# Projecting q one step earlier, spacing a feed-forward, and issuing the second attention's stores from one queue, in a two-layer transformer kernel

## The chip, the cores and the metric

The kernel runs on one core of a Trainium2 chip. The metric is device time in microseconds, from launch to end, median of several runs. The engines are TensorE (PE, with its weight loads shown as PEld), VectorE (DVE), ScalarE (ACT), GpSimd (POOL) and SyncE (SP), which only issues DMAs.

## The reference

The input x has two batches of 1024 rows of 256 features. Two layers follow each other, and each has an attention and a feed-forward; each of the four parts adds the layernorm of its result to x.

```
x = x + LN(L0_attn(LN(x)))   # 16 heads of 128, 1024 keys, weights are codes times block scales
x = x + LN(L0_ffn(LN(x)))    # silu(x Wg * gs) * (x Wu * us) @ Wd * ds, 704 hidden
x = x + LN(L1_attn(LN(x)))   # 16 heads of 16, causal
x = x + LN(L1_ffn(LN(x)))    # 16 experts of 128, top 8 of them weighted, and a shared one of 256
```

## The kernel before, in words

**Precision.** Most operands of a matmul are split into a high and a low 16-bit part: ACT writes the high part, and POOL or DVE subtracts it from the float32 value to give the low part.

**The first attention** sets the pace. `l0_attn` (L704 onward) lists heads of a batch in halves of 512 query rows; a half has four steps, one for each 128 query rows. There are 256 steps in all, 128 for each batch. In step s, `l0_soft` (L627) multiplies q by k into a score tile `pss` of 128x1024, of which there are two; DVE takes the maximum (L631), ACT the exponential `e` (L633). One step later `l0_split` casts it to `hl` (ACT L641, POOL L642) and SP transposes it by DMA into `PT` (L654). Six steps after the scores, `l0_av` (L669) multiplies by v; the result OT goes through `l0_out` (L687).

Each head's projections are put into steps by the function `on`, relative to the first step s of the half that they serve: k (first half only) in steps s-4 and s-3, q in step s-2, v in s+2 and s+3. `l0_qk` is four matmuls (L540) into a tile of `psp` and then the split into two halves: for q, ACT casts (L569 and L572) and POOL subtracts (L573), or ACT and DVE (L545 to L547). q and k have two buffers each. For some heads k and v are stored to DRAM and loaded later for the second half.

**The rest is laid beside it.** `at(step, functions, rate)` puts a list of functions into steps, one each `rate` steps. The feed-forward of the first layer (`ffn`) is such a list for each 512 rows: six times `gu` (gate and up, L873), an empty place, `down` (L889) for the first 256 rows, and the same with two empty places for the others. `down` needs the six hidden tiles `ff_h`, whose low part POOL writes (L881). Three lists are placed at steps 120, 146 (first batch) and 246 (second) at rates of 0.55 and 0.65; the last list runs after the first attention.

The second attention's projections (`l1_qkv`: qk at L981, v at L1019) of the first batch are placed at steps 136 and 160. A qk result is split into a high and low part `l_sq` (`l_sqs` in the second batch), stored to DRAM three times (k as high, high, low; q as high, low, high), and loaded back into `l_k` or `l_q` (L998), stacked so that one matmul does all products of high and low parts. The two copies of the high part are issued by ACT right after its cast (L989); the low part is issued by SP (L992) some ticks later (`QK_LAG`), and the loads a few ticks after that. The work of the second attention itself (`l1_plan`: peaks L1048, scores L1100, `av` L1128) is one list that `between` feeds into the steps at about 1.5 places each from `L1_AT` on. A half begins only when the one before it is through.

**The tail.** After step 256 a planner with made-up time units (`t`) mixes the last feed-forward, the second batch's second attention and the experts (`moe`, L1313 and L1344). `C_FFN` holds the unit at which the last feed-forward begins and its spacing.

**Who orders what.** PE's order is the program's own. On the other engines and in SP's queue a scheduler orders instructions from their place in the program and priorities, so that moving one instruction can reorder others. Every engine works through its instructions in order. SP's queue holds the transposes, loads and stores of everything else too.

Of the kernel before, what the change touches and what calls it, by code (L numbers as in the profile page):

```python
# [22 lines left out]
H0, HD0 = 16, 128  # L23
# [37 lines left out]
L1_W = (100, 104)  # L61
FFN_AT = ((120, 146), 0.55)
FFN1_AT = (246, 0.65)
QKV_AT = ((136, 160), 2.2)
L1_AT = (149, 173)
L1_RATE = (1.6, 1.5)
LAST = 6
EW_AT = (262, 253, 251, 256, 262, 259, 311, 295)
# [5 lines left out]
MOE_LAG = 6  # L74
MUL_DVE = 0.5
C_L1 = 3.2
C_FFN = (20.0, 2.02)
C_QKV = (6.0, 16.0, 3.4)
C_ST = (18.0, 26.0)
C_X3 = 13.09  # L80
# [7 lines left out]
class Net:  # L88
# [615 lines left out]
    def l0_attn(self, filler, between):  # L704


        heads, n, g0 = [], 256, H0 - LAST
        for b in range(B):
            for p, half, hs in ((2 * b, 0, range(g0)), (2 * b, 0, range(g0, H0)), (2 * b, 1, range(H0 - 2, H0)),
                                (2 * b + 1, 1, range(g0, H0 - 2))):  # L710
                for h in hs:
                    heads.append(dict(p=p, b=b, h=h, half=half, PT=[], end=False, keep=g0 <= h < H0 - 2,
                                      w=lambda p=p, h=h: self.wq[p, h // 2]))
                    if h < g0:
                        heads.append(dict(heads[-1], half=1, PT=[]))
                heads[-1]["end"] = p % 2 == 1 or (half == 0 and h == H0 - 1)
        jobs = {}

        def on(s, f):
            jobs.setdefault(s, []).append(f)  # L720

        def tiles(st, *names):
            for x in names:
                if x == "q":
                    st["q"] = self.work.tile([P, 2, 512], F16, name="q", bufs=2)
                else:
                    self.set_kv(st, x, self.new_kv(x))

        deq = {}

        def weights(pair):
            with self.gate():
                deq[pair] = self.l0_weights(pair)

        def reload(ps, pair):
            with self.gate():
                self.l0_reload(ps, pair)

        def reload_o(ps, pair):
            with self.gate():  # L740
                self.l0_reload_o(ps, pair)

        for j, st in enumerate(heads):
            p, h, half, s = st["p"], st["h"], st["half"], 4 * j
            if p % 2 == 1:
                on(s - (5 if h == H0 - 3 else 2), lambda st=st: (tiles(st, "q"), self.l0_qk(st, 0, 1)))
                on(s - 4, lambda st=st: self.kv_load(st, "k"))
                on(s + 2, lambda st=st: self.kv_load(st, "v"))
            elif half == 0:
                on(s - 4, lambda st=st: (tiles(st, "k"), self.l0_qk(st, 1, 0)))  # L750
                on(s - 3, lambda st=st: self.l0_qk(st, 1, 1))
                on(s - 2, lambda st=st: (tiles(st, "q"), self.l0_qk(st, 0, 0)))
                on(s + 2, lambda st=st: (tiles(st, "v"), self.l0_v(st, 0)))
                on(s + 3, lambda st=st: self.l0_v(st, 1))
            else:
                first = heads[j - (1 if h < g0 else 2)]
                on(s - 2, lambda st=st, h0=first: (tiles(st, "q"), self.set_kv(st, "k", h0["k_t"]), self.l0_qk(st, 0, 1)))
                on(s + 3, lambda st=st, h0=first: self.set_kv(st, "v", h0["v_t"]))
            if h % 2 == 0 and (p % 2 or half == 0):
                g = h // 2  # L760
                if p == 0:
                    if g:
                        on(s - 8, lambda g=g: weights(g))
                    for k, dt in enumerate((-6, -5, -2, -1, 2)):
                        if g or k >= 3:
                            on(s + dt, lambda g=g, k=k: deq[g][k]())
                else:
                    on(s - 8, lambda p=p, g=g: reload(p, g))
                    on(s + 1, lambda p=p, g=g: reload_o(p, g))
        on(4 * next(j for j, st in enumerate(heads) if st["h"] == H0 - 2) + 4, self.l0_bias)  # L770
        ready = self.ln_start(self.x0)
        with self.tc.issue_after(ready.ins):
            deq[0] = self.l0_weights(0)
            for f in deq[0][:3]:
                f()
        ps = self.psp.tile([P, 512], F32, name="psp")
        for _ in range(WARM):
            self.nc.tensor.matmul(ps[:, :256], self.zero[:, :P], self.zero[:, :256], start=True, stop=True)
        out_todo = []
        for s in range(-4, n + 3 + L0_LAG + 4):  # L780
            if 0 <= s < n:
                st, qt = heads[s // 4], s % 4
                if qt == 0:
                    st["sum"] = self.small.tile([P, 4], F32, name="sum")
                self.l0_soft(st, qt)
            if 1 <= s <= n:
                self.l0_split(heads[(s - 1) // 4], (s - 1) % 4, s - 1)
            a = s - 3 - L0_LAG
            av = [lambda i=i: self.l0_av(heads[a // 4], a % 4, i) for i in range(2)] if 0 <= a < n else []
            todo = jobs.pop(s, [])  # L790
            if out_todo:
                todo += [f for f in (out_todo.pop(0),) if f]
            if s >= 0:
                todo += filler(s)

            if a % 4 == 0 and av:
                todo = todo[: (len(todo) + 1) // 2] + av[:1] + [lambda: between(s, 0)] + todo[(len(todo) + 1) // 2 :] + av[1:]
            else:
                k = len(todo)
                todo = (todo[: -(-k // 3)] + av[:1] + [lambda: between(s, 0)] + todo[-(-k // 3) : -(-2 * k // 3)]  # L800
                        + av[1:] + todo[-(-2 * k // 3) :])
            for f in todo + [lambda: between(s, 1)]:
                f()
            if av and a % 4 == 3:
                out_todo = [None] * OUT_LAG + [lambda t2=t2, st=heads[a // 4]: self.l0_out(st, t2) for t2 in range(2)]
        assert not jobs, jobs
# [46 lines left out]
    def ffn(self, b, half):  # L853

        nc, w = self.nc, self.work
        st = {}
# [26 lines left out]
        def down(c):  # L883
            ps = self.new_ps()
            for t in range(2):
                for i in range(NI):
                    rows = P if i < 5 else 64
                    for j in range(2):
                        nc.tensor.matmul(ps[:, 256 * t : 256 * t + 256],  # L889
                                         st["h", c, i][:rows, j, t * P : (t + 1) * P], self.fd[:rows, i, :],  # L890
                                         start=(i == 0 and j == 0), stop=(i == NI - 1 and j == 1))
            pv = ps.rearrange("p (t f) -> p t f", t=2)
            y = self.new_y()
            nc.vector.tensor_mul(y, pv, self.ds_bc.unsqueeze(1).to_broadcast([P, 2, D]))
            self.ln_add(1, b, 4 * half + 2 * c, y)

        todo = [lambda i=i: gu(0, i) for i in range(NI)]
        todo += [lambda: None, lambda: down(0)]
        todo += [lambda i=i: gu(1, i) for i in range(NI)]
        return todo + [lambda: None, lambda: None, lambda: down(1)]  # L900


    def l1_weights(self):
# [51 lines left out]
    def l1_qkv(self, b, m):  # L955

        nc, p = self.nc, self.work
        st = {}

        def qk(which, c):  # L960
            n = "qk"[which]
            if b:
                if which == 1:
                    st["sq", c] = p.tile([P, 2, 2, 512], F16, name="l1_sqs", tag="e", bufs=3)
                sq = st["sq", c][:, which, :, :]
            else:
                self.n_sq += 1
                tag, bufs = (("hl_w", 1), ("st", 2), ("st", 2))[self.n_sq % 3]
                sq = p.tile([P, 2, 512], F16, name="l1_sq", tag=tag, bufs=bufs)
            st[n, c] = p.tile([P, 4, 512], F16, name="l1_" + n, bufs=(L1Q_BUFS, 4)[which])  # L970
            if which == 1:
                d = self.k_d1[self.n_kd % 4]
                self.n_kd += 1
            else:
                d = self.dram.tile([2, 50, 4, 512], F16, name="l1_qd", bufs=4)
            ps = self.new_ps()
            col = which * D + m * P
            k = 0
# [5 lines left out]
            bias = self.bqk[:, 2 * which + m : 2 * which + m + 1]  # L984
            self.scaled(sq[:, 0, :], sq[:, 1, :], ps, SC1 / WS1, bias)

            parts = [d[:, 16 * i : 16 * i + 16, :, :].rearrange("g r j t -> g (r j) t") for i in range(3)]
            for i in (0, 2 - which):
                nc.scalar.dma_start(parts[i], sq[:, 0, :])  # L989

            def store():
                self.qk_mark = nc.sync.dma_start(parts[1 + which], sq[:, 1, :])  # L992

            def load():
                rows = 48 + 2 * which
# [4 lines left out]
            todo = [store, load]  # L1000
# [26 lines left out]
        todo = []  # L1027
# [358 lines left out]
    def run(self):  # L1386
        nc, tc = self.nc, self.tc
        with ExitStack() as ctx:
# [62 lines left out]
            for g in range(2):  # L1451
                at(FFN_AT[0][g], self.ffn(0, g), FFN_AT[1])
                at(QKV_AT[0][g], qkv[0, 0][3 * g : 3 * g + 3] + qkv[0, 1][3 * g : 3 * g + 3], QKV_AT[1])
            at(FFN1_AT[0], self.ffn(1, 0), FFN1_AT[1])
# [13 lines left out]
            def between(s, end):  # L1468


                if not end:
                    g = (done[0] >= n_h[0]) + (done[0] >= n_b0)
                    go = g < 2 and s >= L1_AT[g]
                    acc[0] = min(acc[0] + L1_RATE[g], 3.0) if go else 0.0
# [163 lines left out]
```

## Time and profile before

| What | Value |
|---|---|
| Median of three runs | 1785.34 us (1783.87 to 1785.71) |
| The profiled execution's own time | 1787.07 us |
| Its span, first to last instruction | 1785.3 us |
| Mean granted TensorE clock | 0.977 |
| DVE, ACT, POOL busy | 71%, 62%, 50% of the span |
| First attention's scores (L627), first to last | 27.3 to 1247 us |
| Stores of l_sq and l_sqs by ACT / by SP | 32 / 16 |

A profile is one execution. "Busy" counts an engine's own instructions, not its waits or its issuing of DMAs. A wait reads as: engine, tile and line that waited <- engine, tile and line that ended the wait: us in total, times, longest us. PEclk is the share of the full TensorE clock that was granted in a stretch of time.

### The profile page before, as it was taken

Reading aid. Unit: us, or ns where it says so; the run is one execution under the profiler, and the core shown is the slowest. Engines: PE = TensorE matmul, PEld = TensorE weight load, DVE = VectorE, ACT = ScalarE, POOL = GpSimd, SP = SyncE. Lnnn points to the kernel's source line nnn. Section 1 sums busy time; section 2 is a strip of 40 time slices with the busy share of each in tenths; the row PEclk is TensorE's granted clock in tenths of the full one; section 3 lists DMA queues with packets and bytes.
Section 4 is the critical chain, followed back from the end, with each engine's and each line's share of the span. In section 5 each row is a group of like instructions: output and inputs, shape, how many; then the busy total and the mean of one; then the engine's idle time right before and its main releaser. Section 6 shows DMA issues by size and latency. Waiting matters only on the chain.

```text
span 1785.3 us, 35902 instructions
## 1 busy us (share of the span) xinstructions
PE 1608.3 (90%) x13903; PEld 1075.3 (60%) x13903; DVE 1262.1 (71%) x2535; ACT 1109.0 (62%) x1856; POOL 897.0 (50%) x701
## 2 busy tenths in 40 slices
PE   5999999999889888999988889889868898999998
PEld 2566666666556565665555555545656576776877
DVE  5766767676978669565876667886758478775666
ACT  4787787777666655677576777667433444555432
POOL 3666667656666645445445434465343233333444
PEclk9999999999999999999999999999989999999999
DMA  5886988998976975695667766776784322111120
GB/s 125 193 195 156 193 189 184 240 215 179 238 170 164 144 136 117 111 158 128 141 152 179 194 182 152 184 190 162 245 122 105 111 64 67 49 43 45 59 72 13
DMA packets 635316, 257.24 MB, mean 144 GB/s; under 512 B 574916, under 2 KB 615656, under 8 KB 634888
## 3 DMA queue, kind: packets, MB, share of 16 engines
q1 hardware_dynamic: 630984, 250.74, 61.9%
q10 hardware_dynamic: 4160, 4.19, 0.7%
q8 instruction: 109, 1.79, 0.4%
q14 instruction: 63, 0.52, 0.1%
HBM read 76.66 MB, written 35.33 MB: 63 GB/s over the span
## 4 chain that ended last, share of the span: by engine, by line
PE 46%; DVE 24%; ACT 10%; DMA 8%; issue 7%; POOL 2%; SPq 1%; ACTq 0%; DVEq 0%; POOLq 0%
PE pss L627 10%; PE psa L669 9%; PE psp L1313 6%; DVE l_nm L1059 4%; DVE nm L631 4%; PE psp L540 4%; ACT e L633 3%; PE psa L1344 3%; PE psy L1128 2%; ACT hl L641 2%; PE psp L687 2%; DMA pre_ew<-hl_w 2%; PE pss L1100 1%; DVE ln_st L140 1%; PE psp L584 1%
## 5 line engine op out<-in xcount | busy, mean ns | idle before, releaser
L642 POOL TENSOR_TENSOR hl<-e,hl 128x1024 f16<-128x1024 f32 x231 | 492.6, 2133 | 419.9 <-ACT hl L641 315.3
L669 PE MATMUL psa<-PT,v 128*128 128x256 f16 x3072 | 410.9, 275 | 12.4 <-ACT qk L567 11.2
L631 DVE TENSOR_REDUCE nm<-pss 128x1 f32<-128x1024 f32 x256 | 312.0, 1219 | 142.8 <-PE pss L627 142.1
L627 PE MATMUL pss<-k,q 128*128 128x512 f16 x1536 | 379.5, 382 | 35.8 <-ACT e L1112 8.6
L633 ACT ACTIVATE e<-pss,nm 128x1024 f32<-128x1024 f32 x256 | 285.8, 1117 | 128.5 <-DVE nm L631 100.4
L669 PEld LDWEIGHTS <-v 128*128 128x128 f16 x3072 | 296.9, 99 | 105.0 <-issue 28.8
L641 ACT CAST hl<-e 128x1024 f16<-128x1024 f32 x256 | 268.6, 1049 | 13.1 <-DMA PT<-hl 9.7
L627 PEld LDWEIGHTS <-q 128*128 128x128 f16 x1536 | 145.3, 98 | 183.9 <-issue 37.2
L1059 DVE TENSOR_REDUCE l_nm<-pss 128x2 f32<-128x1024 f32 (+3 forms) x152 | 175.8, 1159 | 29.5 <-PE pss L1053 24.9
L1313 PEld LDWEIGHTS <-ew 128*128 128x128 f16 x1728 | 166.1, 99 | 49.6 <-issue 26.3
L1330 POOL TENSOR_TENSOR m_h<-m_t,m_h 128x256 f16<-128x256 f32 x144 | 97.4, 678 | 175.2 <-ACT m_h L1329 173.1
L540 PE MATMUL psp<-xa,wr 128*128 128x512 f16 x488 | 127.9, 386 | 12.6 <-DVE k L552 4.0
L1313 PE MATMUL psp<-xa,ew 128*128 128x256 f16 x1032 | 129.9, 277 | 8.5 <-ACT l_yT L1160 5.1
L1329 ACT CAST m_h<-m_t 128x256 f16<-128x256 f32 x144 | 58.1, 404 | 106.1 <-POOL m_t L1328 40.4
L1320 DVE SCALAR_TENSOR_TENSOR m_t<-m_t,psp 128x256 f32<-128x256 f32 x121 | 50.3, 416 | 95.6 <-ACT m_t L1319 95.1
L573 POOL TENSOR_TENSOR OT<-qk,OT 128x512 f16<-128x512 f32 x64 | 81.3, 1271 | 58.1 <-issue 29.6
L696 DVE SCALAR_TENSOR_TENSOR acc<-psp,r,acc 128x256 f32<-128x256 f32 x224 | 97.1, 474 | 18.9 <-PE psp L687 18.4
L1344 PE MATMUL psa<-ed,m_h 128*128 128x256 f16 x756 | 105.1, 276 | 0.0
L1319 ACT ACTIVATE m_t<-psp 128x256 f32<-128x256 f32 x121 | 46.4, 383 | 89.4 <-PE psp L1313 81.1
L1344 PEld LDWEIGHTS <-m_h 128*128 128x128 f16 x864 | 85.5, 99 | 10.7
L540 PEld LDWEIGHTS <-wr 128*128 128x128 bf16 x512 | 49.4, 99 | 70.1 <-issue 19.0
L1112 ACT ACTIVATE e1x<-pss 128x1024 f32<-128x1024 f32 (+1 forms) x80 | 75.1, 941 | 22.8 <-PE pss L1107 11.8
(221 smaller groups left out, 2637.4 us busy)
## 6 DMA issues: line engine op xcount, KB each, us to landing
cb<-cT_d SPq DMA_DIRECT2D x32, 512.0 KB
w_c<-in_w_codes SPq DMA_DIRECT2D x8, 1024.0 KB
x_d<-y SPq DMA_DIRECT2D x24, 256.0 KB
xr<-x_d SPq DMA_DIRECT2D x24, 256.0 KB
pre_ew<-hl_w SPq DMA_DIRECT2D x18, 256.0 KB
PT<-hl SPq DMA_TRANSPOSE x256
k_d<-k SPq DMA_DIRECT2D x8, 512.0 KB
v_d<-v SPq DMA_DIRECT2D x8, 512.0 KB
```

The lines of the kernel that those rows point to most:

```text
L540: nc.tensor.matmul(ps, w()[:, 1 - which, kt, hs], self.xT[0, st["b"], c][:, :, 2 * j + kt, :], start=(kt == 0 and j == 0), stop=(kt == 1 a ...
L627: nc.tensor.matmul(ps[:, sl], q[:, a, qs], k[:, bb, sl], start=(a == 0 and bb == 0), stop=(a == 1), skip_group_check=True)
L631: self.nm_mark = nc.vector.reduce_max(nm, ps, axis=AX.X, negate=True)
L633: nc.scalar.activation(e, ps, AF.Exp, bias=nm, accum_out=st["sum"][:, qt : qt + 1])
L641: nc.scalar.copy(hl[:, 0, :], e)
L642: (nc.vector if lo_dve else nc.gpsimd).tensor_sub(hl[:, 1, :], e, hl[:, 0, :])
L669: nc.tensor.matmul(ps, v[:, x, kt, :], PT[:, 8 * y + kt, :], start=(kt == 0 and n == 0), stop=(kt == 7 and n == 2))
L696: nc.vector.scalar_tensor_tensor(ys, pv, r, ys, op0=ALU.mult, op1=ALU.add)
L1059: nc.vector.reduce_max(nms[t][:, i % 2, :, j0 : j0 + nj, c], pv, axis=AX.X)
L1313: nc.tensor.matmul(ps[:, 256 * o : 256 * o + 256], self.ew[e][:, o, a, kt, :], xT[:, sl, 2 * x + kt, :], start=(n == 0), stop=(n == 5))
L1330: nc.gpsimd.tensor_sub(h[:, 1, :], th, h[:, 0, :])
L1344: nc.tensor.matmul(py[:, 256 * t : 256 * t + 256], h[:, a, t * P : (t + 1) * P], self.ed[e][:, w, :], start=False, stop=(e == NE - 1 and t ...
```

## The change

Three things. (1) q of a head is projected three steps before its scores instead of two; k one step earlier as well (s-5 and s-4), except for the very first head. (2) Each feed-forward but the last has two more empty places before each `down`; the constants that place the second attention's projections and its start are moved by some steps (`QKV_AT`, `L1_AT`), and the last feed-forward starts 3 planner units later. (3) ACT issues no store of l_sq or l_sqs any more; all three are issued by SP where it issued the low part. Nothing is added to or removed from the arithmetic.

```
-QKV_AT = ((136, 160), 2.2)
-L1_AT = (149, 173)
+QKV_AT = ((138, 166), 2.2)
+L1_AT = (150, 179)
...
-C_FFN = (20.0, 2.02)
+C_FFN = (23.0, 2.02)
...
             if p % 2 == 1:
-                on(s - (5 if h == H0 - 3 else 2), lambda st=st: (tiles(st, "q"), self.l0_qk(st, 0, 1)))
+                on(s - (5 if h == H0 - 3 else 3), lambda st=st: (tiles(st, "q"), self.l0_qk(st, 0, 1)))
...
             elif half == 0:
-                on(s - 4, lambda st=st: (tiles(st, "k"), self.l0_qk(st, 1, 0)))
-                on(s - 3, lambda st=st: self.l0_qk(st, 1, 1))
-                on(s - 2, lambda st=st: (tiles(st, "q"), self.l0_qk(st, 0, 0)))
+                on(max(s - 5, -4), lambda st=st: (tiles(st, "k"), self.l0_qk(st, 1, 0)))
+                on(max(s - 4, -3), lambda st=st: self.l0_qk(st, 1, 1))
+                on(max(s - 3, -2), lambda st=st: (tiles(st, "q"), self.l0_qk(st, 0, 0)))
...
             else:
                 first = heads[j - (1 if h < g0 else 2)]
-                on(s - 2, lambda st=st, h0=first: (tiles(st, "q"), self.set_kv(st, "k", h0["k_t"]), self.l0_qk(st, 0, 1)))
+                on(s - 3, lambda st=st, h0=first: (tiles(st, "q"), self.set_kv(st, "k", h0["k_t"]), self.l0_qk(st, 0, 1)))
...
         todo = [lambda i=i: gu(0, i) for i in range(NI)]
-        todo += [lambda: None, lambda: down(0)]
+        todo += [lambda: None] * (3 - 2 * (b * half)) + [lambda: down(0)]
         todo += [lambda i=i: gu(1, i) for i in range(NI)]
-        return todo + [lambda: None, lambda: None, lambda: down(1)]
+        return todo + [lambda: None] * (4 - 2 * (b * half)) + [lambda: down(1)]
...
-            parts = [d[:, 16 * i : 16 * i + 16, :, :].rearrange("g r j t -> g (r j) t") for i in range(3)]
-            for i in (0, 2 - which):
-                nc.scalar.dma_start(parts[i], sq[:, 0, :])
-
             def store():
-                self.qk_mark = nc.sync.dma_start(parts[1 + which], sq[:, 1, :])
+                for i, a in enumerate((0, 1, 0) if which == 0 else (0, 0, 1)):
+                    self.qk_mark = nc.sync.dma_start(d[:, 16 * i : 16 * i + 16, :, :].rearrange("g r j t -> g (r j) t"), sq[:, a, :])
```

## The prediction

> **What bounds the kernel now.** I read the page's busy line, the 50 us windows, PE's waits, and then the chain and the timelines around the longest ones.
>
> ```profile
> PE 1608.3 (90%) x13903; PEld 1075.3 (60%) x13903; DVE 1262.1 (71%) x2535; ACT 1109.0 (62%) x1856; POOL 897.0 (50%) x701
> ```
>
> TensorE is busy 90% of the span, so only about 177 us of its idle time and what the lowered clock costs can be won; no matmul is removed. The windows say where that time is (start:end, five engines' busy us, then PEclk, DMA share, GB/s):
>
> ```profile
> 250.00:300.00 50.00, 48.08 (x351) 31.69 (x350) 40.08 (x56) 38.98 (x59) 33.55 (x20) 1.00 0.77 176
> 600.00:650.00 50.00, 39.85 (x286) 27.23 (x285) 23.25 (x45) 31.05 (x54) 28.07 (x21) 0.93 1.08 167
> 1300.00:1350.00 50.00, 33.21 (x279) 26.11 (x278) 31.04 (x103) 18.36 (x45) 22.14 (x28) 0.86 0.84 127
> ```
>
> From 100 to 450 us PE idles about 2 us in 100: nothing to win there. The holes are from 450 to 750 (feed-forward and second attention beside the first) and from 1300 to 1350 (just after the first attention ends). PE's waits name the objects of this change:
>
> ```profile
> PE pss L627 <- POOL q L573: 7.3, 8, 1.9
> PE pss L627 <- ACT e L633: 5.3, 7, 1.7
> PE pss L627 <- ACT q L572: 5.2, 4, 2.9
> PE psp L889 <- POOL ff_h L881: 5.0, 4, 3.3
> PE psp L873 <- DMA xb<-ln_hl: 8.1, 2, 6.4
> ```
>
> Scores wait for q 13.1 us (7.3, 5.2, and 0.6 for DVE's q, a smaller row); the weight loader's 19.8 us for q are the same stalls seen from PEld, not counted again. Down projections wait 5.0 for the hidden state. One feed-forward start waits 6.4 for a transpose. A hole also lowers the clock:
>
> ```profile
> 480.00:490.00 10.00, 7.27 (x40) 4.23 (x39) 9.75 (x18) 6.80 (x11) 8.54 (x6) 0.83 1.05 270
> 510.00:520.00 10.00, 8.82 (x42) 4.80 (x43) 5.01 (x15) 1.80 (x4) 1.13 (x2) 0.66 0.63 146
> ```
>
> The first holds a 1.9 us wait for q, the second the 3.3 us wait for ff_h. Mean clocks of 0.83 and 0.66 over 10 us are 1.7 and 3.4 us of matmul time lost behind the stall.
>
> [...]
>
> **The change, part by part.** One step of the first attention is (1247 - 27.3) / 256 = 4.77 us, from its first and last L627.
>
> *q three steps ahead (k four and five).* A projection is the same four matmuls (0.87 us), moved; also moved are its ACT, DVE and POOL operations, and k's store on SP. The built programs' order shows q's ACT cast one exponential earlier in nearly every head: q moves by one step, 4.8 us, against a longest wait of 2.9. Head 0 keeps its step, and its waits at 27 and 28 us (1.3 us) stay: 11.8 us can go. What is late next is the score buffer, freed by the exponential: L627's waits for e are 5.3 us in 7, or 0.76 each. If each of the 11 remaining stalls turns into one, 8.4 stay and 3.4 go, and 1.7 of clock at 480 us. I take **5.1**, between 0 (e was as late as q) and 13.5. That v and the first k now share a step is no cost: over eight steps PE has the same matmuls. ACT's wait for k (76 us in 49, L551) should shorten, off the path while ACT is 62% busy.
>
> *Two more empty steps before each down projection, in three of the four feed-forwards.* The chain at 507 us shows POOL's ff_h behind ln_hl (1.14) and hl (2.08). Two places at 0.55 are 1.1 steps, 5.2 us, more than the longest wait of 3.3. So 5.0 go, with half of the 3.4 of clock: **6.7**, bounds 0 and 8.4. Nothing behind is late: the results come 1.1 and 2.2 steps later, and the second attention's projections are moved 2 and 6 steps to match.
>
> *Second attention shifted.* In PE's order its first half starts at step 151 instead of 150; its second, which waits for the first half's end, at 184 instead of 183. Two feed-forward units and two of its score units cross into the tail. PE's sum is unchanged: **0**, bounds -3 and 3, about what those units are long.
>
> *The last feed-forward 3 units later in the tail.* PE's order has one more expert unit ahead of its first matmul: 12 matmuls of L1313 (1.30 us) and 6 of L1344 (0.66). That fills **2.0** of the 6.4 us wait at 1311 us; bounds 0 and 6.4.
>
> *All stores from SP.* ACT issued 32 stores at medians of 0.50 to 0.74 us, 18 us in all, some far longer. The ACT and PE timelines (start, us, engine, line, idle before):
>
> ```profile
> 1400.47 4.93 ACTq L989 DMA_DIRECT2D l_kd<-l_sqs  x2
> 1405.44 0.37 ACT L1160 COPY l_yT<-psp 128x256 f32<-128x256 f32 x1 [5.90 <-issue]
> ```
> ```profile
> 1405.87 2.72 PE L1313 MATMUL psp<-xa,ew 128*128 128x256 f16 x12 [3.74 <-ACT l_yT L1160]
> ```
>
> Two issues held ACT for 5 us and PE for 3.74. Likewise PE waited 1.95 us at 1316.6 (ACT's qk) and 3.94 at 1325.1 (ACT's v, behind a copy that stood 6.1 us for the l_qd issue): 9.6 us together, and 2.6 of clock at 1400 (0.74). The stores now stand on SP, ahead of the loads and the xb transposes, so half the waits may return: I take 4.8 + 2.6 = **7.4**, bounds 0 and 13.9 (all of it, and the 1.7 that 0.83 at 1320 costs).
>
> *What SP pays.* 32 more issues at about 0.53 us are 17 us of its time, and it issues in order. Behind each store stand the transposes of hl (L654), for which av waits. A store of three issues delays one by 1.6 us; the transpose has some four steps (19 us) till av. The bad place is a load right behind the store it reads:
>
> ```profile
> SPq L998 <- DMA l_kd<-l_sq: 11.9, 2, 8.3
> ```
>
> SP stood 8.3 us for one landing. Before, this stood once in the first batch's order; in the changed order three times (first q, third and fourth k). Two more are 16.6 us of standing SP, mostly under that cover: I take **-3**, bounds 0 and -24 (below).
>
> [...]
>
> Sum: 5.1 + 6.7 + 0 + 2.0 + 7.4 - 3 = 18.2 us. The profiled execution took 1787.07 (span 1785.3), 1.7 above the median of 1785.34: 1787.1 - 18.2 - 1.7 = **1767**.
>
> **The rivals.** *SP becomes late (slower).* The price is in the trace. After two qk groups' stores and loads met at 610 us, the chain holds this piece, and PE starved:
>
> ```profile
> 613.02 20.07 DMA PT<-hl x2
> ```
> ```profile
> 620.00:630.00 10.00, 5.80 (x34) 4.01 (x35) 1.60 (x3) 5.88 (x11) 6.28 (x4) 0.83 1.35 147
> 630.00:640.00 10.00, 5.31 (x55) 4.70 (x54) 3.51 (x7) 5.39 (x10) 5.65 (x4) 0.84 0.68 162
> ```
>
> PE waited 3.8 us at 623.6 and 4.7 at 637.0, and two clock drops cost 3.3: 11.8 per collision. Two more, at the two places where a load now stands behind its store, cost 23.6; with the 11.8 won on q and down projections the net is 11.8 slower: 1787.1 + 11.8 - 1.7 = 1797. It decides once a transpose is late by more than its 19 us, which takes a standing SP of 8.3 us and a backlog as at 613. For it: transposes there took 5 to 10 us to issue against a median of 1.6. Against it: the DMA share of 1.35 came with two queues in flight; one queue may spread that, and elsewhere the new order puts a transpose between store and load.
>
> *The waits only change names.* The scores wait for e where they waited for q, SP's stalls reach PE through the loads, and only the down projections' 5.0 us go, less 3 for SP: 1783. For it: the L627 waits for e and e1x, already some 19 us.
>
> *The change does not do what it says:* excluded for q, k and the feed-forward by the built order; the L1 constant for the second half alone is nearly idle, as that half is bound by the first.
>
> **How the numbers follow.** A measurement here can tell about 0.2% (3.6 us) from no change. The forecast gets 0.57, all faster. "Names only" gets 0.14, of which 0.08 within 0.2% and 0.06 faster. SP late gets 0.29, slower. Faster 0.63, same 0.08, slower 0.29. The low end takes q 13.5, down 8.4, ACT 13.9 and tail 2.0 at their bounds, 37.8: 1747. The high end is the SP rival, 1797. Some 0.1 lies beyond each. The forecast alone would span 1747 to 1781.
>
> **What would show it.** Right: L627's waits for q under 3 us, L889's for ff_h near 1, no ACT stall at a store's issue, a mean clock above 0.977, 600:650 no worse than 40 us of PE. Wrong: more PE wait on psa or ACT qk at L567 between 570 and 800 us, SP's waits for l_kd and l_qd above the 56 us before, or the wait of L873 for xb not shrinking.

## The result and the profile after

The changed kernel takes 1801.54 us (median of four runs, 1797.93 to 1803.09), the kernel before 1784.61 beside it. The ratio is 1.0094, 95% interval 1.0075 to 1.0113: 17 us slower, where 18 us faster was forecast. The profiled execution took 1801.62 (span 1799.9, mean clock 0.968).

In the changed kernel all lines behind the stores are numbered 3 lower (L1100 is L1097, L1025 is L1022). The busy line and the three windows of the prediction read now:

```profile
PE 1614.6 (90%) x13903; PEld 1077.6 (60%) x13903; DVE 1257.1 (70%) x2535; ACT 1115.3 (62%) x1856; POOL 894.2 (50%) x701
```
```profile
250.00:300.00 50.00, 49.73 (x353) 32.51 (x351) 36.77 (x58) 39.83 (x61) 32.61 (x20) 1.00 0.74 162
600.00:650.00 50.00, 43.92 (x338) 30.08 (x338) 32.97 (x55) 38.06 (x65) 32.90 (x25) 0.97 0.79 138
1300.00:1350.00 50.00, 36.52 (x323) 28.80 (x323) 31.99 (x113) 19.62 (x46) 24.76 (x31) 0.90 0.68 141
```

The same 13,903 matmuls take 6.3 us more (1608.3 to 1614.6), and PE's time without a matmul grows by 8.3 (177.0 to 185.3, span less busy): together the 14.6 us between the two spans. So in these two executions a good part of the loss is clock, not waiting; the mean clock was 0.966 to 0.971 in all four executions of the changed kernel. And these three windows are *better* than before (48.08, 39.85 and 33.21 then). So are three of the four short ones that the prediction had named for their stalls and low clock (8.82, 5.80 and 5.31 then); the first, 7.27 then, is not:

```profile
480.00:490.00 10.00, 6.86 (x38) 4.03 (x37) 9.86 (x15) 6.39 (x10) 5.87 (x5) 0.89 0.84 205
510.00:520.00 10.00, 10.00 (x72) 6.69 (x72) 7.27 (x14) 9.14 (x16) 8.89 (x9) 1.00 1.15 219
620.00:630.00 10.00, 10.00 (x77) 6.65 (x76) 3.59 (x5) 8.87 (x16) 6.30 (x4) 1.00 1.22 215
630.00:640.00 10.00, 9.77 (x81) 6.98 (x79) 7.01 (x15) 7.96 (x16) 8.46 (x8) 1.00 0.79 102
```

The loss is in other places:

```profile
800.00:850.00 50.00, 42.53 (x373) 25.64 (x371) 21.00 (x39) 30.08 (x46) 17.56 (x11) 0.93 0.67 133
```
```profile
1350.00:1400.00 50.00, 42.15 (x513) 30.52 (x508) 39.28 (x118) 18.11 (x39) 15.26 (x19) 0.90 0.32 99
1400.00:1450.00 50.00, 40.06 (x409) 26.95 (x408) 26.69 (x76) 20.53 (x38) 13.24 (x16) 0.87 0.36 100
```

Before, PE was busy 48.92, 45.21 and 43.19 us in these three. The last L627 ends at 1248 us in both kernels, though two feed-forward units and two score units have left that stretch; what follows it is 14 us longer. PE's waits have changed their names. Of the prediction's five rows (waits for q 7.3 and 5.2, for e 5.3, for ff_h 5.0, for xb 8.1) these are left, grown or new:

```profile
PE pss L1045 <- ACT e L633: 16.2, 12, 4.6
PE pss L1097 <- DMA l_q<-l_sT: 12.0, 4, 6.0
PE pss L627 <- ACT e L633: 10.0, 11, 2.1
PE pss L889 <- ACT ff_hs L880: 9.3, 1, 9.3
PE psp L687 <- POOL OT L573: 9.0, 9, 1.9
PE psp L540 <- DVE wr L479: 7.9, 3, 3.4
PE pss L627 <- ACT q L572: 1.1, 1, 1.1
PE psp L873 <- DMA xb<-ln_hl: 0.4, 1, 0.4
PE pss L627 <- POOL q L573: 0.2, 1, 0.2
```

The scores' waits for q are 1.3 us, xb's 0.4: the change does what the forecast said it would. In their place stand waits for e, for the decoded weights `wr` (none before in front of L540), for `OT` and, most of it in the tail, two waits for what SP loads (`l_q` directly; `ff_hs` by way of DVE, as shown below). Of the waits for e the first row has grown most: the second attention's peaks wait 16.2 us for a score tile (5.9 before, L1048 there). The scores' own row for e nearly doubled, but with the second attention's exponentials, which free the same tiles, L627's waits fell from 19.1 to 16.0 us.

### The profile page after: what moved, and what is told of

It is laid out like the page before. It is cut to its first block, busy times and chain, and to the rows that moved or that the text cites. A ratio compares the mean times of both kernels' runs of the same rounds, so it can differ in the third digit from the quotient of the medians.

```text
span 1799.9 us, 35928 instructions
## 1 busy us (share of the span) xinstructions
PE 1614.6 (90%) x13903; PEld 1077.6 (60%) x13903; DVE 1257.1 (70%) x2535; ACT 1115.3 (62%) x1856; POOL 894.2 (50%) x701
## 5 line engine op out<-in xcount | busy, mean ns | idle before, releaser
L669 PE MATMUL psa<-PT,v 128*128 128x256 f16 x3072 | 414.2, 277 | 12.1 <-ACT qk L567 8.9
L627 PE MATMUL pss<-k,q 128*128 128x512 f16 x1536 | 381.4, 385 | 20.3 <-ACT e L633 10.0
L669 PEld LDWEIGHTS <-v 128*128 128x128 f16 x3072 | 297.8, 99 | 107.9 <-issue 28.5
L641 ACT CAST hl<-e 128x1024 f16<-128x1024 f32 x256 | 267.8, 1047 | 20.4 <-DMA PT<-hl 16.7
L627 PEld LDWEIGHTS <-q 128*128 128x128 f16 x1536 | 147.5, 99 | 167.9 <-issue 39.3
L540 PE MATMUL psp<-xa,wr 128*128 128x512 f16 x492 | 128.3, 384 | 16.2 <-DVE wr L479 7.9
L540 PEld LDWEIGHTS <-wr 128*128 128x128 bf16 x512 | 48.5, 98 | 74.6 <-issue 13.3
```

Of the source, the lines that this page charges most:

```text
L540: nc.tensor.matmul(ps, w()[:, 1 - which, kt, hs], self.xT[0, st["b"], c][:, :, 2 * j + kt, :], start=(kt == 0 and j == 0), stop=(kt == 1 a ...
L627: nc.tensor.matmul(ps[:, sl], q[:, a, qs], k[:, bb, sl], start=(a == 0 and bb == 0), stop=(a == 1), skip_group_check=True)
L641: nc.scalar.copy(hl[:, 0, :], e)
L669: nc.tensor.matmul(ps, v[:, x, kt, :], PT[:, 8 * y + kt, :], start=(kt == 0 and n == 0), stop=(kt == 7 and n == 2))
```

## The experiments

All numbers are ratios to the kernel before, run on the same chip beside it, with the 95% interval; "us" is the ratio less one, times 1784.6. Times of stretches come from one execution each, and 19 executions of the kernel before on one chip spread from 1777.6 to 1791.3: a few us in a stretch of one trace are not a finding.

### The three parts alone

`q_only` is part 1 of the diff in the change section (q and k), `ffn_only` part 2 (empty places and constants), `stores_only` part 3. `after_act_stores` is the changed kernel with the stores back as they were.

> Only q and k projected one step earlier. Theory SP (the stores on SP's queue cost the 17 us, in the tail): 1780 to 1786, the waits for q gone, with new waits for wr eating part of it. Theory projections (the earlier k and q meet weights that are not yet made, 7.9 us of waits for wr in the changed kernel, and lower the clock): 1790 to 1798. Theory order (no part has a cost of its own, any reordering moves the time by some 10 us): anything from 1775 to 1800.

> Only the empty steps in the feed-forwards and the shifted constants. Theory SP: 1778 to 1785, down projections without waits. Theory projections: the same. A third possibility, that the later feed-forward and second attention push work into the tail, where PE waits more: 1788 to 1795.

> Only the stores moved from ACT to SP. Theory SP: 1795 to 1800, with PE waiting at L1100 for l_q<-l_sT and for x3 loads between 1300 and 1450 us. Theory projections: 1780 to 1787, as ACT's stalls at 1316, 1325 and 1405 us (9.6 us of PE) become SP's.

> The changed kernel, with the two stores of the high part back on ACT. Theory SP: 1775 to 1786. Theory projections: 1797 to 1803, since the first attention is as it was in the changed kernel.

| run | ratio | us |
|---|---|---|
| q_only | 1.0129 (1.0098 to 1.0161) | +23 |
| ffn_only | 1.0092 (1.0061 to 1.0123) | +16 |
| stores_only | 0.9944 (0.9908 to 0.9979) | -10 |
| after_act_stores | 1.0108 (1.0075 to 1.0140) | +19 |

Two of the three parts lose, and one alone, the stores, beats both kernels (median 1773.84 us; 4 to 16 us by the interval). Six of all the runs were slower than every range written down for them, by 3 us or more: q_only, ffn_only, after_act_stores, k_early, q_four and k_early_weights. The parts don't add: 23 + 16 is 39, both together cost 19; and the stores' 10 us shrink to 2 (1.0108 against 1.0094, within the intervals) once the other two are there.

### Part 1: it is k, not q

```
# q_early: q at s-3 as in the change, k left at s-4 and s-3
# k_early: q left at s-2, and
-                on(s - 4, lambda st=st: (tiles(st, "k"), self.l0_qk(st, 1, 0)))
-                on(s - 3, lambda st=st: self.l0_qk(st, 1, 1))
+                on(max(s - 5, -4), lambda st=st: (tiles(st, "k"), self.l0_qk(st, 1, 0)))
+                on(max(s - 4, -3), lambda st=st: self.l0_qk(st, 1, 1))
# q_four: q at s-4, k as before
```

> Only q one step earlier, k where it was. Theory OT step: 1797 to 1810, PE's waits at L669 for ACT's qk at 18 us or more, and q's cast between the end of psa and its copy in 30 or more of the 64 halves. Theory weights: 1780 to 1788.

> Only k one step earlier, q where it was. Theory OT step (q now stands in the step in which ACT copies the finished av tile psa out, and its cast, for which ACT waits on PE, delays that copy, so that the next av waits): 1780 to 1788, PE's waits at L669 for ACT's qk near the 11 us of before. Theory weights (k meets weights made only one step before): 1793 to 1808, with 7 to 8 us of waits for wr at L540 and the lowered clock behind them.

> q four steps ahead, k as before. Theory OT step, reduced to what q_early showed (13 us of waits for q gone, 20 us more of waits of L669 for ACT's qk): one step further q no longer shares OT's step, so the waits for psa go back to about 11 and those for q stay away, 1770 to 1780. Rival order: 1783 to 1795, the waits move to another name again.

q_early: 1.0007 (0.9988 to 1.0025), +1 us. k_early: 1.0167 (1.0137 to 1.0197), +30. q_four: 1.0092 (1.0069 to 1.0116), +16.

For q, these are rows of PE's waits in q_early; before they were 11.2 in 9, 2.6 in 4 and 5.3 in 7:

```profile
PE psa L669 <- ACT qk L567: 30.6, 27, 4.2
PE psp L687 <- POOL OT L573: 6.1, 7, 1.6
PE pss L627 <- ACT e L633: 6.8, 8, 2.4
```

Adding PE's idle gaps up to the last L627 by what it was to write next: in front of the scores they fall from 35.7 to 12.6 us, in front of av's `psa` they rise from 11.9 to 32.9, in front of L687 from 8.1 to 14.7. With q alone moved, what is late next is not the score buffer, as the prediction had it, but `psa`. It has one copy out, on ACT (L567), in the step in which q's casts now stand. The longest of these waits, ACT's timeline and then PE's (start, us, engine, line, idle before):

```profile
622.88 0.61 ACT L572 CAST l_sq<-qk 128x512 f16<-128x512 f32 x1
623.52 1.66 ACTq L989 DMA_DIRECT2D l_qd<-l_sq  x2
625.29 1.11 ACT L633 ACTIVATE e<-pss,nm 128x1024 f32<-128x1024 f32 x1 [1.80 <-POOL hl L642]
626.30 0.19 ACT L633 ACTIVATION_READ_ACCUMULATOR e<-pss,nm 128x1 f32 x1
626.39 0.68 ACT L569 ACTIVATE qk<-psp,bqkv 128x512 f32<-128x512 f32 x1
626.96 0.59 ACT L567 ACTIVATE qk<-psa 128x512 f32<-128x512 f32 x1
```
```profile
627.61 1.01 PE L669 MATMUL psa<-PT,v 128*128 128x256 f16 x4 [4.24 <-ACT qk L567]
```

Two store issues, a late exponential and q's bias step (L569) stand ahead of the copy, and PE stands 4.24 us for it. In this place it had stood 3.80 us before, behind the store issues without q's bias step: the row shows the order on ACT, and the growth is in the number, 27 for 9. Over the 64 copies of a trace, ACT started 18 casts (L572) and 9 bias steps of q between the end of a `psa` and its copy in q_early, and none before. The cast of `hl` (L641, 1.05 us) moved there too, 27 times for 2: from the end of a `psa` to its copy pass 97 us in all for 72, of which q's operations (with five casts of L545) take 20 and `hl`'s 28. The scheduler's new order on ACT is as much of the cause as q's own casts. q_four moves q out of that step: `psa` falls back to 15.2 us, but those of `psp` before L687 grow to 16.0 (6.9 before), and the half-clock time of the first attention from 41.0 to 61.4. Neither of the two earlier places tried is better for q than the one it had. In the whole change the successor is another again: `psa`'s waits are 8.9 us there, and PE's idle time in front of L687, which needs `OT`, goes from 8.1 to 21.2.

For k, the waits that k_early brings are these (not one of them stood in front of L540 before):

```profile
PE psp L540 <- DVE wr L479: 8.1, 7, 2.8
```
```profile
802.75 1.89 PE L540 MATMUL psp<-xa,wr 128*128 128x512 f16 x4 [5.04 <-DMA wr<-w_d]
```

The weights of a pair of heads are decoded by PE and DVE (L477, L479), k's at s-6 and q's at s-5, and k's first half used them at s-4. At s-5 it stands one step behind them: seven waits, 33 to 60 us apart, once for each pair of heads. In the second batch the weights are reloaded from DRAM, and that load is late once. These 13 us explain less than half of the 30. In this trace PE idles 21 us longer than before and is busy 1 us longer, so the loss is waiting and not clock. Of the idle time 10 us more stand in front of L540; the rest is spread over L873 (4.0 more up to the last L627), av (3.3), three lines of the second attention (8.1) and L687 (2.4), with 5.0 less in front of L1019. The next runs asked for it.

```
# k_early_weights: k_early, and the making and reload of the weights one step earlier
-                        on(s - 8, lambda g=g: weights(g))
-                    for k, dt in enumerate((-6, -5, -2, -1, 2)):
+                        on(s - 9, lambda g=g: weights(g))
+                    for k, dt in enumerate((-7, -6, -2, -1, 2)):
-                    on(s - 8, lambda p=p, g=g: reload(p, g))
+                    on(s - 9, lambda p=p, g=g: reload(p, g))
# k_second: only k's second half one step earlier, s-4 instead of s-3
# k_early_b1: k earlier in the second batch alone
# k_b1_reload: k_early_b1, and that batch's reload at s-10 instead of s-8 (up to head 10)
```

> k one step earlier as in k_early, and the weights' loading, their scaling of wk and wq, and the reloads one step earlier too. Theory weights: 1780 to 1792, L540's waits for wr (DVE and DMA) back under 3 us. Rival psp (k's first half now shares a step with v's second, and the two psp tiles turn over too slowly): 1800 to 1815 as k_early, with waits of L540, L584 and L687 for DVE's v and k.

> Only k's second half one step earlier, in the same step as the first half, which stays at s-4; so no projection meets its weights earlier than before. Theory weights (the first half of k at s-5 meets wk made at s-6): 1780 to 1790 and no waits for wr at L540. Rival crowding (k earlier fills the step's psp tiles and ACT): 1797 to 1812.

> Both halves of k one step earlier, in the second batch only, where wr comes by DMA. Theory weights: 1785 to 1797, with the 5 us wait for wr<-w_d near 800 us and nothing else new. Rival crowding: 1797 to 1808, since most of what k_early lost by the trace came between steps 128 and 184, in the second batch beside the second attention.

> k is made a step earlier in the second batch only, as in k_early_b1 (1.0085), and the reload of the projection weights for that batch is issued a step earlier too. Theory that the loss there is the late weights (the 4.7 us wait near 798 us): the wait is gone and the time falls to 1783 to 1791 us. Rival, that the loss is the projection standing among other projections and feed-forward steps: the wait goes or shrinks, and the time stays at 1794 to 1802 us.

k_early_weights: 1.0229 (1.0199 to 1.0259), +41. The waits of L540 for DVE's `wr` are gone, but the weight making itself now waits (L477 for `wr` 11.7 us, 4.9 before), and the half-clock time of the first attention is 75.1 us against 51.2 in k_early. So the late weights are not the whole reason, and moving their making along only moves the trouble. k_second: 1.0042 (1.0022 to 1.0062), +7: by this most of the loss is the first half's. k_early_b1: 1.0085 (1.0066 to 1.0103), +15, half of the loss for half of the heads, with one named wait. SP's timeline shows why the load is late (a transpose of 8.69 and one of 5.49 us stood ahead of it), PE's what it costs:

```profile
776.25 8.69 SPq L654 DMA_TRANSPOSE PT<-hl  x1
786.38 5.49 SPq L654 DMA_TRANSPOSE PT<-hl  x1
791.92 0.58 SPq L517 DMA_DIRECT2D wr<-w_d  x1
```
```profile
798.36 1.89 PE L540 MATMUL psp<-xa,wr 128*128 128x512 f16 x4 [4.72 <-DMA wr<-w_d]
```

k_b1_reload takes that wait away: no L540 waits for `wr` there any more. It still measures 1.0115 (1.0070 to 1.0160), no faster than k_early_b1. So the late load is at most a small part of the loss in the second batch, unless moving the load cost elsewhere what it saved here. Smaller waits stand in that stretch instead (behind ACT's qk 1.8 us, DVE's acc 1.8, DVE's k 1.1); the placing of k beside other steps' work is what is left, argued and not shown: no run tells which neighbour it is.

### Part 2: every piece costs a little

```
# ffn_start20: part 2, but C_FFN = (20.0, 2.02) as before
# start23:     only C_FFN = (23.0, 2.02)
# ffn_b0:      empty places in the first batch's two lists, shift of QKV_AT and L1_AT, start 20
# ffn_b1:      empty places in the third list alone, all constants as before
# l1_shift:    only QKV_AT = ((138, 166), 2.2) and L1_AT = (150, 179)
```

> The empty steps in the feed-forwards and the shifted second attention, but the last feed-forward starts at 20 as before. Theory tail start (the 3 units later are what costs the 8 us of the tail beyond the work pushed there): 1783 to 1790. Theory pushed chain (the second attention's later end delays what the tail waits for): 1796 to 1804 as with 23.

> Only the start of the last feed-forward at 23 in place of 20. Everything up to 1247 us is as before. Theory tail start: 1792 to 1800. Theory pushed chain: 1780 to 1787, with the 6.4 us wait of L873 for xb smaller.

> The empty steps in the first batch's two feed-forwards only, with the shifted second attention; last feed-forward at 20. Theory late third (the third feed-forward, at step 246, ends 2.6 steps later, while the tail's second batch of qk and v, which read its result, keep their place): 1780 to 1788. Rival pushed second half (second attention one step later is what the tail waits for): 1794 to 1802.

> The empty steps in the third feed-forward only (second batch, first half); all constants as before. Theory late third: 1790 to 1800, with PE waiting for ACT's v, xb or qk between 1300 and 1340 us. Rival pushed second half: 1781 to 1788.

> Only the moved constants of the second attention (QKV_AT, L1_AT); feed-forwards as before. Theory shift (the later second attention meets fewer free places, and its end delays the tail): 1792 to 1800. Rival spacing (the empty steps themselves cost): 1780 to 1788.

| run | ratio | us |
|---|---|---|
| ffn_start20 | 1.0073 (1.0051 to 1.0095) | +13 |
| start23 | 1.0028 (1.0007 to 1.0048) | +5 |
| ffn_b0 | 1.0067 (1.0044 to 1.0090) | +12 |
| ffn_b1 | 1.0023 (1.0001 to 1.0045) | +4 |
| l1_shift | 1.0034 (1.0021 to 1.0046) | +6 |

The shift costs 6; by subtraction the empty places of the first batch cost about as much again (12 - 6), the third list's 4, the later start 3 to 5. Added up that is 19 to 21 where the part costs 16; with intervals of some 4 us each way on most of them, the difference says nothing. The late third list, which one theory had as the main cost, is 4 of it: ffn_b0 loses 12 without it. The waits for ff_h in the first attention did go (5.0 before; in ffn_start20 0.2). But L873 waits longer in the tail (for v 3.9, ff_t 0.9 and xb 6.4 before), and the second attention's projection L981, near 580 us, meets a feed-forward result that is not there yet. Rows of ffn_start20:

```profile
PE psy L981 <- DMA xb<-ln_hl: 6.9, 1, 6.9
PE psy L873 <- ACT v L1025: 10.4, 1, 10.4
PE psp L873 <- DVE ff_t L879: 4.9, 4, 1.7
PE psp L873 <- DMA xb<-ln_hl: 4.3, 1, 4.3
```

The wait of L981 is 6.9 to 7.0 us in ffn_only, ffn_start20 and ffn_b0, and stands neither in the kernel before nor in l1_shift, ffn_b1 or the whole change. SP issues the transpose that it waits for at 563.4 us before, 560.5 in l1_shift and 576.8 in ffn_b0, 13 us later than before, while the projection was moved by two steps, some 9.5 us. In ffn_only and ffn_start20 the first attention is hardly shorter (1242 and 1246 us against 1248, though work has left it), with 58 us of it at half clock against 41, and the tail takes 553 and 552 us against 538.

### Part 3: the stores, and where their gain lies

```
# stores_first: all stores from SP in the first batch, the second batch's by ACT and SP as before
# stores_q_early: part 3 and q at s-3
```

> All stores of q and k are issued from SP in the first batch only; the second batch's keep the split between ACT and SP. Theory that what the stores gain lies in the first attention's stretch 535 to 720 us: 1775 to 1780 us. Rival, that it lies in the tail, where ACT's stalls at 1300 to 1410 us go: 1780 to 1786 us.

> All stores on SP, and q alone one step earlier, k as before. Theory swap (q's waits come back as psa's): 1768 to 1780, no better than the stores alone. Rival addition (with ACT free of stores OT's copy is no longer late): 1755 to 1767.

stores_first: 0.9976 (0.9957 to 0.9995), -4 us; stores_only had -10. By the medians about half of the gain lies in each batch, between the two theories; the intervals overlap, so the share is not shown. stores_q_early: 0.9974 (0.9956 to 0.9992), -5: q's earlier place adds nothing that shows to the stores. In stores_only the windows of both places are better than the 39.85, 33.21 and 45.21 before:

```profile
600.00:650.00 50.00, 45.28 (x336) 30.95 (x334) 27.40 (x50) 35.59 (x60) 30.22 (x22) 0.97 0.91 160
1300.00:1350.00 50.00, 37.80 (x380) 29.04 (x377) 37.94 (x116) 17.47 (x43) 20.98 (x28) 0.90 0.62 121
1350.00:1400.00 50.00, 47.55 (x592) 33.67 (x593) 35.55 (x102) 27.17 (x53) 17.53 (x21) 1.00 0.38 117
```

The ACT waits of the prediction's store term (L1313 for l_yT 3.74, L873 for v 3.94, L1019 for qk 1.95) and psa's 3.8 at 623.6 are gone or at most 1.0 us. Two waits are new (the second was 0.2 us before):

```profile
PE psy L873 <- DVE y L894: 6.2, 1, 6.2
PE pss L1097 <- DMA l_q<-l_sT: 5.4, 1, 5.4
```

In the first, DVE stands 8.77 us for a load of `y` up to 1319.65; both are read in the changed kernel below, and only the second turns out to be SP's price.

## Why the prediction was wrong, point by point

**q (5.1 us): right wait, wrong successor, and no gain.** The waits for q went, as said. The step that failed is "what is late next is the score buffer ... 0.76 each". Alone, q's 13 stalls became 2, those of head 0, and `psa`'s 9 became 27. The working looked at which buffer the *scores* need, and not at which engine gets the moved casts, what else that engine owes PE in the new step, and what the scheduler does with the rest of its work. Alone q gives +1 us. (One step is 4.76 us by the division given there, and the low end 1747.6; nothing rests on either.)

**k (priced at nothing): the largest miss, +30 alone.** "That v and the first k now share a step is no cost: over eight steps PE has the same matmuls" counts PE's load only. It left out where k's input comes from: its weights are made two steps before it, and it was moved to one step behind them. q may hide some of this (+23 with q early, +30 without; the intervals overlap). Of the 30, the named waits are 13; two runs that each removed a part of them by other means did not get the time back. That the late weights are the main cost is therefore not shown; that k's place is, is.

**Empty places (6.7 us): the wait went, the time did not.** "Nothing behind is late" is the step that failed. In the runs with the first batch's empty places the transposed result comes 13 us later, where the prediction had 1.1 and 2.2 steps (5 and 10 us) and moved the projection by two; PE stands 6.9 to 7.0 us for it at L981. In the whole change this wait is gone, and no run tells what it became. In the third list the second batch's projections are not moved along (`C_QKV` stays); that list costs 4. **The shift (0, bounds -3 and 3)** costs 6, beyond its bound. **The later last feed-forward (2.0 gained)** costs 5 alone, and here the step was right: in start23's trace the 6.4 us wait for xb is 4.5. But behind it the wait of L1019 for ACT's qk grows from 1.9 to 4.7 us: the next wait took its place, and the term had counted only the first.

**Stores (7.4 less 3 for SP): right in sign and mechanism.** Alone they give 10 us (4 to 16) where the net said 4.4. The total of 18 us for ACT's issues was read too low, medians times 32: the 32 took 25.4 us. Inside the whole change about 2 us of gain are left, within the intervals. Of the two new waits the larger, for `y`, looks like SP's price and is mostly not. In the changed kernel at the tail's start, the timelines of SP, DVE, ACT and PE:

```profile
1320.01 0.40 SPq L339 DMA_DIRECT2D x_d<-y  x1
1320.50 4.28 SPq L989 DMA_DIRECT2D l_kd<-l_sqs  x3
1324.99 2.33 SPq L194 DMA_DIRECT2D y<-x_d  x1
```
```profile
1333.58 0.75 DVE L140 BATCH_NORM_STATS2 ln_st<-y 128x6 f32<-128x256 f32 x2 [8.70 <-DMA y<-x_d]
1334.67 0.38 DVE L878 SCALAR_TENSOR_TENSOR ff_t<-ff_t,psy 64x256 f32<-64x256 f32 x1
1336.01 0.41 ACT L880 CAST ff_hs<-ff_t 64x256 f16<-64x256 f32 x1 [0.91 <-DVE ff_t L879]
1336.47 0.39 PE L889 MATMUL pss<-ff,ff_hs 64*128 64x256 bf16 x1 [9.34 <-ACT ff_hs L880]
```

And DVE in the kernel before, where nothing waits for that load:

```profile
1331.52 0.74 DVE L140 BATCH_NORM_STATS2 ln_st<-y 128x6 f32<-128x256 f32 x2
```

DVE stands idle for 8.70 us at L140 for the load. Behind it on DVE is the last hidden tile of the feed-forward, whose input ACT had ready at 1324.5, and behind that PE, 9.34 us. Three stores, 4.28 us of issue, stand between the store of `x_d` and the load. But the load reads what that store writes, and starts at its landing, 1324.93, which comes after the last of the three is issued. It does so before as well (landing 1319.84, load 1319.86): the stores fill a wait that is there anyway. From the store of `x_d` to the landing of `y` pass 13.6 us in the changed kernel and as much in after_act_stores, 13.4 in stores_only and 15.5 before. The load's own part is 8.6 us in the changed kernel and 5.6 in after_act_stores, which is the most that the stores can have slowed it. What has changed is when DVE comes to L140: at 1324.9, in stores_only at 1310.9, and before at 1331.5, after waits of 10.40 and 5.37 us for `ff_t` from ACT. So this is the next link, laid open by the gain on ACT. In stores_only other work is queued behind it, and PE pays 6.2 us.

The wait for `l_q` is SP's price: 5.4 us in stores_only, 12.0 in the changed kernel, 9.3 of them in the tail; SP's timeline, then PE's:

```profile
1392.13 6.32 SPq L989 DMA_DIRECT2D l_kd<-l_sqs  x3
1398.55 3.19 SPq L1083 DMA_DIRECT2D l_q<-l_sT  x2
1438.17 0.79 SPq L995 DMA_DIRECT2D l_q<-l_qd  x2
1439.47 1.34 SPq L1083 DMA_DIRECT2D l_q<-l_sT  x2
```
```profile
1406.60 0.75 PE L1097 MATMUL pss<-l_q,l_k 50*128 50x256 f16 x4 [3.38 <-DMA l_q<-l_sT]
1444.30 1.19 PE L1097 MATMUL pss<-l_q,l_k 50*128 50x256 f16 x8 [5.96 <-DMA l_q<-l_sT]
```

ACT had the first `l_sT` ready at 1393.3; its load came 5.2 us later, as the third store's issue alone took 4.96. The second, which is the one of stores_only, was ready at 1430.6 and came 8.9 us later: SP was issuing a load of `l_k`, and then stood 4 us, to 1438.1, for the landing of the stores of `l_qd`. Before, both loads came within 0.5 us of `l_sT`. So the term of 3 was 5.4 alone. Why the gain falls from 10 to 2 beside the other parts no run tells; the two waits are 11.6 us alone and 21.3 there.

**The SP rival (1797)** came near the number by luck, as the part that it was to sink, the stores, is the only one that gains. Half of its mechanism is real: SP does become late. But its place, 600 to 650 us, got better, and SP's waits for l_qd and l_kd are 51.2 us in all where more than 56 was the sign. What is late in the tail are two loads of `l_q`, one behind the issue of stores and one behind a landing, and no transpose. Nearest to the rival's own picture is the stretch between 790 and 830 us, where SP stood 14.2 us for landings, in the window whose PE fell from 48.92 to 42.53.

**What would show it.** Five signs of "right" were named. L627 for q under 3: held (1.3). L889 for ff_h near 1: held in the first attention. No ACT stall at a store's issue: held. 600:650 no worse than 40: held (43.92). Mean clock above 0.977: failed (0.968). Four of five held and the forecast was wrong: only the clock is taken over the whole span, the others all look at what the change was meant to remove. None of the three signs of "wrong" came either: PE's wait for ACT's qk at L669 between 570 and 800 us fell from 3.8 to 1.5, SP's waits fell from 56 to 51.2, and the wait for xb from 8.1 to 0.4.

**The clock.** The prediction credited 6 us of clock to removed stalls. The opposite came: 85.6 us at half clock before in 18 stretches, 116.1 in 23 after (the granted clock in all of these is 0.5; stores_only 72.6 in 16; some 2 us of each lie past the end of the span). The 30 us more at half clock go with the 6.3 us by which the same matmuls take longer. The traces also show what stands ahead of a stretch. In each of the two all begin on one grid of 3.41 us, and in the grid window just ahead PE's matmuls were busy 0 to 54% of the time before, 0 to 47% after. Of the other windows at full clock from the first L627 on, none is under 42% (471 of them, before) or 45% (462, after). So in these two traces the drops go with the idle time in a window, not with the length of one wait: ahead of 486.7 us two waits for q, 0.82 and 1.91, left PE busy 30% of one. By the median of each run's executions, the mean clock fell most with the first batch's empty places (0.968 in ffn_only and ffn_b0) and less with part 1 (0.974 in q_only), and not with the stores (0.978; 0.976 to 0.978 in the kernel before).

**What stays open.** Why k's earlier place costs 17 us more than the waits with its name; why parts 1 and 2 together cost 20 us less than their sum; how much of the 6 us of the first batch's empty places is the wait at L981. In this kernel PE's order is fixed, and each piece changes which steps coincide; the runs show the price of each piece, not the neighbour that makes it.

## What to carry to other kernels

Before an operation is moved earlier, list three things at its new place and not only the wait it removes: who makes its inputs and when (k's weights), which engine gets its follow-up work and what else that engine owes there (q's casts ahead of the copy of `psa`), and what stands behind it in a queue (the stores ahead of the loads of `l_q`). When a new wait shows behind a faster engine, look whether its cause is new or was covered before (the load of `y`). In this schedule, busy 90% and tuned by hand, "the same matmuls, moved" cost 0.1 to 2.3% and never gained; take that into the range. Run the parts apart: here one part of three was a gain of 0.6% that the other two hid.

## What the runs showed of the hardware that was not expected

The clock drops come in whole stretches of 3.4 us at a granted clock of 0.5 (of the 18 before, 12 are 3.4 us, four 6.8, one 10.2 and one 7.1; of the 23 after, 13 are 3.4, eight 6.8, one 10.2 and one 6.9; the odd one is the last, which runs past the end). A window need not be idle here for the clock to fall: as worked out above, one that was busy up to 54% went ahead of a stretch, and none under 42% went without.

The price of issuing a store varied tenfold: one issue at L989 took 0.49 us at best and 3.62 at worst on ACT before, and up to 4.97 on SP after. Of the nine over 2 us (three before, six after) seven are in the second batch; why they are long no run shows. Moving 32 stores from ACT to SP gained 10 us (4 to 16) alone: the 32 issues had taken 25.4 us of ACT's time, and some stood ahead of work that PE waited for, 3.74 us at 1405.87. On SP it costs too where a load stands behind it: PE's 3.38 us for `l_q`.
